# Two attention layers on one core: first-layer products alternate between query halves, first keys come from SBUF, residuals load within the block

## Chip, cores and metric

The kernel runs on one core of a Trainium2 chip. The metric is the device time of one execution in microseconds (us). Engines are named as the profile names them: PE is the tensor engine (its weight loads are shown apart, as PEld), DVE the vector engine, ACT the scalar engine, POOL GpSimd, SP the engine that issues most DMAs. SBUF and PSUM are the on-chip memories; PSUM has eight banks, and matmuls accumulate there.

## What is computed

Four images of 64 x 64 pixels and 256 channels go through two self-attention layers, each over an image's 4096 pixels ("tokens"). Cut to what matters:

```python
# layer 0
q = x @ Wq + bq;  k = x @ Wk + bk;  v = x @ Wv + bv        # 32, 32, 256 wide
x = gamma * (softmax(q @ k.T) @ v) + x
# layer 1
f = x @ Wf + bf;  g = x @ Wg + bg;  v = x @ Wh + bh        # 32, 32, 128 wide
x = x + (softmax(g @ f.T) @ v) @ Wo + bo
```

## The kernel before

**Blocks and steps.** For each image, layer 0 goes through 16 blocks of 256 queries and, within a block, through 8 steps of 512 keys. Layer 1 goes through 8 blocks of 512 queries with 16 steps of 256 keys. One object `Step` stands for one step, and a single loop (L658) goes through all of them in order.

**A step of layer 0.** `scores` (L495) makes four matmuls of 128 keys by 256 queries into the tile `st`, the only one of its kind, two PSUM banks. ACT turns it into `high` (an exponential with a slightly lowered argument, rounded to fp32r) and `p` (the plain exponential). DVE makes `low = p - high` (`cut_low`, L516) and `d` from `low` and `high` (`cut_both`, L521). These three parts of one probability are multiplied with three forms of the values, `v0h`, `v0l`, `v0d`, so that the sum has full precision from matmuls that PE takes in one go. `products_first` (L528) does this for one half `s` (128 of the 256 queries) and one part: four matmuls, one for each 128 keys (`g`), whose weights are a 128-column piece of the part and whose moving tile is `v0[..][:, g, :]`, 258 columns. A block has four accumulators of one PSUM bank each: `acc[0]` and `acc[1]` for half 0 (high and low into the first, `d` into the second), `acc[2]` and `acc[3]` for half 1. A plain step makes 24 products: high of half 0, high of half 1, low of half 0, low of half 1, then the scores of the step after next, then `d` of both halves (L714 to L724). The last step of a block has another order, so that half 0 is done early.

**The end of a block.** In layer 0, `end_first` (L563) has ACT copy `acc[0]` and `acc[2]` (L569), DVE adds `acc[1]` and `acc[3]` (L570); the next block's accumulators take these banks. In layer 1, `end_second` (L597) has ACT copy one accumulator, DVE add the other (L604), and DVE fold the running sum `p_sum` (L700) into `sums`. What follows is a list of "units": `begin` issues the loads of two residual tiles (`x_old`, from the DRAM tensor `x1_res`), `nothing` is a pause, and four `output(t)` each make two matmuls (L623, L624), a reciprocal, a DVE instruction that scales and adds the residual (L628), the store of the result, and the load of the residual tile two further on.

**Units and their pace.** Besides the outputs, units are the projections: a unit that transposes 512 tokens (in image 0 on PE, later on DVE), one for queries and keys (`qk_unit`, L408), and two to four for values (`psv`, L437). The loop spreads a block's units over its steps (L704 to L707), so a shorter list puts each unit earlier. A planner that models times orders the instructions of each engine in the end; within an engine they run in that order.

**Queries and keys.** `qk_unit` leaves `qk_parts` in SBUF (one buffer), 128 rows: high and low parts of 32 rows of q and 32 of k. SP writes it to DRAM (L428, `qk_dram`); `load_k` (L472) and `load_q` (L465) read four pieces of 32 rows back with DMAs from POOL into the tiles `k` and `q`. In image 0 the first three projections (`AHEAD`) come ahead of all steps, and the other five during the first block, three steps ahead of the step that uses them.

**Small tiles.** Residuals, outputs and other tiles of 128 x 256 share one pool `small` of four buffers.

Of the kernel before, what the change touches and what calls it, by code (L numbers as in the profile page):

```python
# [50 lines left out]
F32R = mybir.dt.float32r  # L51
# [5 lines left out]
P = 128  # L57
QB = 512
QB0 = 256
# [174 lines left out]
def fast_path(ctx: ExitStack, tc: tile.TileContext, x, w0, w1, wo, bo, gamma, out, off):  # L234
# [170 lines left out]
    def project_units(b, l, j):  # L405
        key = (b, l, j)

        def qk_unit():  # L408
            ps = side_psum(f"psqk_{b}_{l}_{j}")
            for c in range(NCC):  # L410
                for n in range(2):
                    nc.tensor.matmul(  # L412
                        ps,
                        wqk[l][:, c, :],
                        x_parts[key][c][n],
                        start=(c == n == 0),
                        stop=(c == NCC - 1 and n == 1),
                    )
            whole = data.tile([2 * D, QB], F32, tag="qk", name=f"qk_{b}_{l}_{j}")
            parts = data.tile([P, QB], F32R, tag="qk_parts", name=f"qk_parts_{b}_{l}_{j}")  # L420
            top, bottom = slice(0, 2 * D), slice(2 * D, P)
            nc.scalar.copy(whole, ps[bottom, :])  # L422
            nc.vector.scalar_tensor_tensor(whole, ps[top, :], bqk[l], whole, ALU.add, ALU.add)  # L423
            nc.scalar.copy(parts[top, :], whole)
            nc.vector.tensor_sub(parts[bottom, :], whole, parts[top, :].bitcast(F32))

            qk_dram[key] = dram.tile([2, 2, D, QB], F32, name=f"qk_dram_{b}_{l}_{j}")
            nc.sync.dma_start(qk_dram[key].rearrange("h w d n -> (h w d) n"), parts.bitcast(F32))  # L428

        per = QB // CV[l]  # L430

        def v_unit(t0):
            def issue():
                ps = side_psum(f"psv_{b}_{l}_{j}_{t0}").rearrange("p (t c) -> p t c", c=CV[l])
                for t in range(per):
                    for c in range(NCC):
                        nc.tensor.matmul(  # L437
                            ps[:, t, :],
                            xT[key][:, c, (t0 + t) * P : (t0 + t + 1) * P],
                            wv[l][:, c, :],  # L440
                            start=(c == 0),
                            stop=(c == NCC - 1),
                        )
                tiles = slice(t0, t0 + per)
                seen = [seen_v[:, l, b * NB + j, n : n + 1] for n in range(2)]
                if l == 0:
                    split_values(ps, *(v0[j][what][:, tiles, :C] for what in ("h", "l", "d")), seen[t0 // per])
                    return
                for n in range(NT // G[1]):
                    i = j * NT // G[1] + n  # L450
                    v = ps[:, n * G[1] : (n + 1) * G[1], :]
                    if split[1][i]:
                        t = data.tile([P, 3, G[1], P], F32R, tag="v1_parts", bufs=sum(split[1]), name=f"v_{b}_{i}")
                        v_t[b, i] = {what: t[:, m] for m, what in enumerate(("h", "l", "d"))}
                        split_values(v, *v_t[b, i].values(), seen[n])
                    else:
                        v_t[b, i] = data.tile([P, G[1], P], F32, tag="v1", bufs=V1, name=f"v_{b}_{i}")
                        nc.scalar.copy(v_t[b, i], v)
                        nc.scalar.activation(v, v, AF.Abs, accum_out=seen[n])

            return issue

        return [transpose_unit(b, l, j), qk_unit] + [v_unit(t0) for t0 in range(0, NT, per)]

    def load_q(b, l, j):  # L465

        q_t[b, l, j] = data.tile([P, QB], F32R, tag="q", bufs=2, name=f"q_{b}_{l}_{j}")
        for n in range(4):
            src = qk_dram[b, l, j][n // 2, 0].bitcast(F32R)
            nc.gpsimd.dma_start(q_t[b, l, j][n * D : (n + 1) * D, :], src)  # L470

    def load_k(b, l, j):  # L472

        k_t[b, l, j] = data.tile([P, QB], F32R, tag="k", bufs=NB, name=f"k_{b}_{l}_{j}")
        for n in range(4):
            src = qk_dram[b, l, j][n % 2, 1].bitcast(F32R)
            nc.gpsimd.dma_start(k_t[b, l, j][n * D : (n + 1) * D, :], src)  # L477

    def nothing():
        pass  # L480
# [5 lines left out]
    class Step:  # L486
# [38 lines left out]
                    self.d, self.low.bitcast(F32), -1.0 / EPS, self.high.bitcast(F32), ALU.mult, ALU.add  # L525
                )

        def products_first(self, acc, s, what):  # L528
            p, v, which = {
                "h": (self.high, "h", 0), "l": (self.low, "l", 0), "d": (self.d, "d", 1)  # L530
            }[what]
            for g in range(G[0]):
                nc.tensor.matmul(  # L533
                    acc[2 * s + which][:, :W],
                    p[:, g * QB0 + s * P : g * QB0 + (s + 1) * P],
                    v0[self.i][v][:, g, :],
                    start=self.first and what != "l" and g == 0,
                    stop=self.last and what != "h" and g == G[0] - 1,
                )

        def products_second(self, acc):
            v = v_t[self.b, self.i]
# [20 lines left out]
    def end_first(b, j, acc):  # L563
# [30 lines left out]

        return [residual(0), residual(1)]

    def end_second(b, j, acc, p_sum):  # L597
        key = f"{b}_{j}"
        o = []
        for h in range(QB // QB0):  # L600
            part = slice(h * QB0, (h + 1) * QB0)
            o.append(work.tile([P, W], F32, tag="o", name=f"o_{key}_{h}"))
            nc.scalar.activation(o[h][:, :QB0], acc[0][:, part], AF.Copy, scale=1.0 + EPS)
            nc.vector.tensor_add(o[h][:, :QB0], o[h][:, :QB0], acc[1][:, part])  # L604
        sums = work.tile([P, QB], F32, tag="sums", bufs=1, name=f"sums_{key}")
        nc.vector.tensor_add(sums, p_sum[:, :QB], p_sum[:, QB:])
        x_old = {}

        def load(t):
            if t < NT:  # L610
                x_old[t] = small(f"x1_old_{key}_{t}")
                nc.sync.dma_start(x_old[t], x1_res[b, j][t * P : (t + 1) * P, :])

        def begin():
            load(0)
            load(1)

        def output(t):
            def issue():
                tok = slice(t * P, (t + 1) * P)  # L620
                ps = side_psum(f"pso_{key}_{t}")
                part = o[t // NS][:, t % NS * P : (t % NS + 1) * P]
                nc.tensor.matmul(ps[:, :C], part, wo_sb, start=True, stop=True)  # L623
                nc.tensor.matmul(ps[:, C : C + 1], sums[:, tok], ones[:, :1], start=True, stop=True)  # L624
                n = (b * N + j * QB) // P + t
                nc.vector.reciprocal(inverse[:, 1, n : n + 1], ps[:, C : C + 1])
                y = small(f"y_{key}_{t}")
                nc.vector.scalar_tensor_tensor(y, ps[:, :C], inverse[:, 1, n : n + 1], x_old[t], ALU.mult, ALU.add)  # L628
                row = j * QB + t * P
                nc.sync.dma_start(out[b, row : row + P, :], y)  # L630
                load(t + 2)

            return issue

        return [begin, nothing] + [output(t) for t in range(NT)]

    def run(units):
        for u in units:
            u()


    x_res = {}
    for j in range(AHEAD):
        run(project_units(0, 0, j))
        load_k(0, 0, j)
        if j == 0:
            load_q(0, 0, 0)

    steps = [Step(b, l, j, i) for b in range(B) for l in range(2) for j in range(NQ[l]) for i in range(NI[l])]
    steps[0].scores()  # L650
# [7 lines left out]
    for n, s in enumerate(steps):  # L658
# [15 lines left out]
        if l == 0 and s.last:  # L674
            x_res[b, j] = []
            for t in range(NS):
                x_res[b, j].append(small(f"x_res_{b}_{j}_{t}"))
                row = (j * NS + t) * P
                nc.sync.dma_start(x_res[b, j][t], x[b, row : row + P, :])
                nc.gpsimd.tensor_add(x_res[b, j][t], x_res[b, j][t], bv)  # L680

        ahead = steps[n + 3] if n + 3 < len(steps) else None
        if ahead is not None and ahead.first:
# [25 lines left out]
        if l == 1:  # L709
            later.scores()  # L710
            run(todo)
            s.products_second(acc)
        else:
            for half, what in ((0, "h"), (0, "l"), (1, "h")) if s.last else ((0, "h"), (1, "h")):  # L714
                s.products_first(acc, half, what)
            for half in () if s.last else (0, 1):
                s.products_first(acc, half, "l")
            run(early[1:])
            if early:
                load_k(0, 0, s.i + AHEAD)  # L720
            later.scores()
            run(todo)
            for half, what in ((0, "d"), (1, "l"), (1, "d")) if s.last else ((0, "d"), (1, "d")):
                s.products_first(acc, half, what)  # L724

        over = (min(s.i + 2, NI[l] - 1) + 1) * G[l] // NT if j == NQ[l] - 1 else 0
        while keys and keys[0] in qk_dram and (keys[0][:2] == (b, l) or keys[0][2] < over):
# [73 lines left out]
```

## Time and profile before

| | |
|---|---|
| median of 4 runs | 3233.61 us (3231.79 to 3236.5) |
| profiled execution | 3235.59 us, of which the span of the profile is 3233.7 us |
| layer-0 block of image 1 to 3 | 27.0 to 29.2 us, by the starts of ACT's copies L569 |
| layer-1 block | 41.6 us; 37.35 us in the last image, which has no projections for a next image beside it |
| first layer-0 product of image 0; of image 1 | 33.5 us; 868.3 us |
| last layer-1 product | 3216.3 us |

A page of the profile gives, for each engine, its busy time and the number of its instructions, then the span in 40 slices with the busy share in tenths, and the clock that PE was granted. The chain that ended last names what set the end; groups of instructions are given by line, engine and tile (`acc<-v0h,high` is a matmul that reads `v0h` and has `high` as weights). In the timeline a row has its start, its length and how many instructions were merged into it; matmuls are pipelined, so the rate is read from starts, not from lengths. "Idle before" names who ended a wait.

### The profile page before, as it was taken

The numbers are of one execution on the slowest core, as the hardware profiler recorded it, in microseconds if no ns is written. First come the engines' busy times: TensorE is split into PE (matmuls) and PEld (weight loads), VectorE is DVE, ScalarE is ACT, GpSimd is POOL, SyncE is SP. The second block draws the span as 40 slices with busy tenths as digits, with TensorE's granted clock in tenths as the row PEclk, the third lists the DMA queues.
The fourth block names the chain that finished last, engine by engine and source line by source line (L and its number), as shares of the span: only waits on it lengthen the run. The fifth ranks groups of instructions, "written<-read, shape, count | busy, mean of one in ns | idle before, by whom it ended". The sixth has DMA issues, their size and how long they took to land. (4 is left out here: it accounts for less than half of the span.)

```text
span 3233.7 us, 51123 instructions
## 1 busy us (share of the span) xinstructions
PE 3172.4 (98%) x19460; PEld 2619.4 (81%) x19460; DVE 2684.5 (83%) x3181; ACT 1989.0 (62%) x2483; POOL 660.4 (20%) x784
## 2 busy tenths in 40 slices
PE   8999999999999999999999999999999999999998
PEld 7999997566699999656679999966668999995554
DVE  6788888888888888788888888878888888887776
ACT  6666666555566666565556666655555666665554
POOL 2222223000222222300022222310002222241000
PEclk9999999999999999999999999999999999999999
DMA  3112123222212112322121212222222211121111
GB/s 116 42 48 50 44 56 75 56 53 49 62 44 56 42 47 51 77 56 51 47 64 43 50 47 52 61 64 51 51 54 61 53 42 48 43 70 47 33 33 36
DMA packets 368652, 172.15 MB, mean 53 GB/s; under 512 B 257392, under 2 KB 343664, under 8 KB 368400
## 3 DMA queue, kind: packets, MB, share of 16 engines
q1 hardware_dynamic: 342528, 134.29, 16.0%
q0 software_dynamic: 24960, 34.18, 4.6%
q8 instruction: 157, 2.57, 0.3%
q14 instruction: 95, 0.78, 0.1%
q10 hardware_dynamic: 912, 0.33, 0.0%
HBM read 101.58 MB, written 67.11 MB: 52 GB/s over the span
## 5 line engine op out<-in xcount | busy, mean ns | idle before, releaser
L514 ACT ACTIVATE p<-st 128x1024 f32<-128x1024 f32 x1024 | 1044.6, 1020 | 388.3 <-PE st L502 383.3
L512 ACT ACTIVATE high<-st,down 128x1024 fp32r<-128x1024 f32 x608 | 678.7, 1116 | 691.4 <-PE st L502 573.0
L524 DVE SCALAR_TENSOR_TENSOR d<-low,high 128x1024 fp32r<-128x1024 f32 x608 | 761.2, 1252 | 209.3 <-PE acc L533 203.6
L519 DVE TENSOR_TENSOR low<-p,high 128x1024 fp32r<-128x1024 f32 x608 | 808.7, 1330 | 141.0 <-ACT p L514 141.0
L554 PE MATMUL acc<-p,v 128*128 128x512 f32 x1664 | 791.7, 598 | 0.0
L502 PE MATMUL st<-q,k 128*128 128x256 f32 (+1 forms) x3072 | 776.8, 361 | 11.4 <-ACT p L514 11.2
L700 DVE TENSOR_TENSOR p_sum<-p_sum,p 128x1024 f32<-128x1024 f32 x480 | 586.5, 1222 | 59.0 <-ACT p L514 50.7
L502 PEld LDWEIGHTS st<-q,k 128*128 128x128 f32 x3072 | 463.7, 189 | 208.6 <-ACT p L514 114.7
L533 PE MATMUL acc<-v0d,d 128*128 128x258 f32 x4096 | 592.3, 284 | 0.1
L533 PE MATMUL acc<-v0h,high 128*128 128x258 f32 x4096 | 588.5, 284 | 3.1 <-ACT high L512 3.0
L533 PE MATMUL acc<-v0l,low 128*128 128x258 f32 x4096 | 588.2, 283 | 2.3 <-DVE low L519 2.3
L533 PEld LDWEIGHTS acc<-v0h,high 128*128 128x128 f32 x4096 | 533.9, 190 | 5.3 <-ACT high L512 3.8
L533 PEld LDWEIGHTS acc<-v0d,d 128*128 128x128 f32 x4096 | 533.9, 190 | 4.8 <-DVE d L524 1.6
L533 PEld LDWEIGHTS acc<-v0l,low 128*128 128x128 f32 x4096 | 532.9, 190 | 3.9 <-DVE low L519 3.7
L554 PEld LDWEIGHTS acc<-p,v 128*128 128x128 f32 x1664 | 309.8, 190 | 226.8 <-issue 199.4
L590 POOL TENSOR_TENSOR x_res<-x,bo 128x256 f32<-128x256 f32 x128 | 215.2, 1681 | 860.4 <-DVE g L580 482.6
L470 POOL DMA_DIRECT2D q<-qk_dram x256 | 125.9, 503 | 1167.4 <-PE st L502 1145.4
L680 POOL TENSOR_TENSOR x_res<-x_res,bv 128x256 f32<-128x256 f32 x128 | 189.9, 1484 | 146.9 <-DMA x_res<-in_x 100.1
L437 PE MATMUL psv<-wv,xT 128*128 128x128 f32 (+1 forms) x1024 | 193.4, 333 | 6.7 <-DVE qk L423 6.1
L477 POOL DMA_DIRECT2D k<-qk_dram x256 | 125.2, 499 | 303.2 <-DMA qk_dram<-qk_parts 159.9
L437 PEld LDWEIGHTS psv<-wv,xT 128*128 128x128 f32 x1024 | 160.4, 193 | 30.0 <-DVE qk L423 8.7
L388 DVE TENSOR_TENSOR xl<-xT,xh 128x512 fp32r<-128x512 f32 x128 | 87.0, 682 | 4.3 <-ACT xh L387 3.9
(94 smaller groups left out, 1676.4 us busy)
## 6 DMA issues: line engine op xcount, KB each, us to landing
x_res<-in_x SPq DMA_DIRECT2D x128, 128.0 KB, 2.2
qk_dram<-qk_parts SPq DMA_DIRECT2D x64, 256.0 KB, 2.1
k<-qk_dram POOLq DMA_DIRECT2D x256, 64.0 KB, 2.1
q<-qk_dram POOLq DMA_DIRECT2D x256, 64.0 KB, 2.1
x_dram<-x SPq DMA_DIRECT2D x128, 128.0 KB, 1.7
x_res<-x_res SPq DMA_DIRECT2D x128, 128.0 KB, 1.7
squares<-x_dram SPq DMA_DIRECT2D x256, 64.0 KB, 2.3
x_old<-x_res SPq DMA_DIRECT2D x128, 128.0 KB, 2.1
```

Source lines behind the costliest of these rows:

```text
L437: nc.tensor.matmul(ps[:, t, :], xT[key][:, c, (t0 + t) * P : (t0 + t + 1) * P], wv[l][:, c, :], start=(c == 0), stop=(c == NCC - 1),)
L470: nc.gpsimd.dma_start(q_t[b, l, j][n * D : (n + 1) * D, :], src)
L502: nc.tensor.matmul(st[:, g, :], k_t[b, l, kt // NT][:, kt % NT * P : (kt % NT + 1) * P], q_t[b, l, j * n // QB][:, q0 : q0 + n], start=Tru ...
L512: nc.scalar.activation(self.high, s_flat, AF.Exp, bias=down)
L514: nc.scalar.activation(self.p, s_flat, AF.Exp)
L519: nc.vector.tensor_sub(self.low, self.p, self.high.bitcast(F32))
L524: nc.vector.scalar_tensor_tensor(self.d, self.low.bitcast(F32), -1.0 / EPS, self.high.bitcast(F32), ALU.mult, ALU.add)
L533: nc.tensor.matmul(acc[2 * s + which][:, :W], p[:, g * QB0 + s * P : g * QB0 + (s + 1) * P], v0[self.i][v][:, g, :], start=self.first and ...
L554: nc.tensor.matmul(acc[which], v[:, g, :], p[:, g * QB : (g + 1) * QB], start=first and g == 0, stop=last and g == G[1] - 1,)
L590: nc.gpsimd.tensor_add(x_old[s], x_new[s], bo_sb)
L680: nc.gpsimd.tensor_add(x_res[b, j][t], x_res[b, j][t], bv)
L700: nc.vector.tensor_add(p_sum, p_sum, s.p)
```

## The change

1. `products_first` takes a list of halves. In plain steps it is called for both halves at once, and the loop over halves is the inner one: for each 128 keys first half 0, then half 1. The last step of a block keeps its order.
2. In image 0's layer 0, `load_k`, and for the first tile `load_q`, are called within `qk_unit` and read `qk_parts` in SBUF instead of `qk_dram`. The write to DRAM stays. The calls after each projection go.
3. `load_old` loads all four residual tiles of a layer-1 block at its step 12 into four `small` tiles; the result is written in place of the residual. `begin`, `nothing` and the loads within `output` go.

```diff
@@ qk_unit
             nc.sync.dma_start(qk_dram[key].rearrange("h w d n -> (h w d) n"), parts.bitcast(F32))
+            if b == l == 0:
+                near = parts.rearrange("(h w d) n -> h w d n", h=2, w=2)
+                load_k(b, l, j, near)
+                if j == 0:
+                    load_q(b, l, j, near)
@@ loads
+    def load_rows(dst, parts, which, halves):
+        for n, h in enumerate(halves):
+            nc.gpsimd.dma_start(dst[n * D : (n + 1) * D, :], parts[h, which])
+
-    def load_k(b, l, j):
+    def load_k(b, l, j, parts=None):
         k_t[b, l, j] = data.tile([P, QB], F32R, tag="k", bufs=NB, name=f"k_{b}_{l}_{j}")
-        for n in range(4):
-            src = qk_dram[b, l, j][n % 2, 1].bitcast(F32R)
-            nc.gpsimd.dma_start(k_t[b, l, j][n * D : (n + 1) * D, :], src)
+        load_rows(k_t[b, l, j], qk_dram[b, l, j].bitcast(F32R) if parts is None else parts, 1, (0, 1, 0, 1))
@@ Step
-        def products_first(self, acc, s, what):
+        def products_first(self, acc, halves, what):
...
             for g in range(G[0]):
-                nc.tensor.matmul(
-                    acc[2 * s + which][:, :W],
-                    p[:, g * QB0 + s * P : g * QB0 + (s + 1) * P],
+                for s in halves:
+                    nc.tensor.matmul(
+                        acc[2 * s + which][:, :W],
+                        p[:, g * QB0 + s * P : g * QB0 + (s + 1) * P],
...
@@ layer 1
+    def load_old(b, j):
+
+        x_old[b, j] = []
+        for t in range(NT):
+            x_old[b, j].append(small(f"x1_old_{b}_{j}_{t}"))
+            nc.sync.dma_start(x_old[b, j][t], x1_res[b, j][t * P : (t + 1) * P, :])
+
@@ end_second
-        def begin():
-            load(0)
-            load(1)
-
...
-                nc.vector.scalar_tensor_tensor(y, ps[:, :C], inverse[:, 1, n : n + 1], x_old[t], ALU.mult, ALU.add)
+                nc.vector.scalar_tensor_tensor(y[t], ps[:, :C], inverse[:, 1, n : n + 1], y[t], ALU.mult, ALU.add)
...
-                load(t + 2)
...
-        return [begin, nothing] + [output(t) for t in range(NT)]
+        return [output(t) for t in range(NT)]
@@ the loop
+        if l == 1 and s.i == NI[1] - 4:
+            load_old(b, j)
...
-            for half, what in ((0, "h"), (0, "l"), (1, "h")) if s.last else ((0, "h"), (1, "h")):
-                s.products_first(acc, half, what)
-            for half in () if s.last else (0, 1):
-                s.products_first(acc, half, "l")
+            both = range(NS)
+            order = [((0,), "h"), ((0,), "l"), ((1,), "h")] if s.last else [(both, "h"), (both, "l")]
+            for halves, what in order:
+                s.products_first(acc, halves, what)
             run(early[1:])
-            if early:
-                load_k(0, 0, s.i + AHEAD)
             later.scores()
             run(todo)
-            for half, what in ((0, "d"), (1, "l"), (1, "d")) if s.last else ((0, "d"), (1, "d")):
-                s.products_first(acc, half, what)
+            for halves, what in [((0,), "d"), ((1,), "l"), ((1,), "d")] if s.last else [(both, "d")]:
+                s.products_first(acc, halves, what)
```

## Prediction

> **What bounds the kernel now.** I read the page first: busy shares, the clock row, the chain. Then busy time by stage, then the timeline of one layer-0 block boundary, of one layer-1 block, of the first 105 us and of the tail.
>
> ```profile
> PE 3172.4 (98%) x19460; PEld 2619.4 (81%) x19460; DVE 2684.5 (83%) x3181; ACT 1989.0 (62%) x2483; POOL 660.4 (20%) x784
> ...
> PEclk9999999999999999999999999999999999999999
> ```
>
> TensorE is busy nearly always at full clock, so an edit pays only if it shortens a matmul or fills a hole on PE. By stage (us, busy time and instructions of each engine, granted clock, DMA share, GB/s):
>
> ```profile
> 0.00:15.00 15.00, 10.25 (x28) 6.86 (x28) 5.89 (x63) 6.30 (x13) 7.85 (x18) 1.00 0.74 228
> 15.00:33.50 18.50, 15.16 (x64) 11.05 (x64) 11.75 (x18) 12.44 (x26) 8.04 (x17) 0.91 0.52 143
> ...
> 86.00:101.70 15.70, 11.18 (x69) 10.00 (x68) 8.29 (x9) 8.21 (x12) 1.94 (x4) 0.89 0.13 34
> ...
> 868.30:1320.00 451.70, 451.70 (x3732) 449.63 (x3731) 384.90 (x434) 293.33 (x357) 126.16 (x122) 1.00 0.20 50
> 525.00:868.00 343.00, 335.12 (x1111) 201.46 (x1110) 286.13 (x346) 200.60 (x258) 36.64 (x70) 0.99 0.24 58
> ```
>
> A later image's layer 0 (868 to 1320) has no hole at all: PE 451.70 of 451.70. Layer 1 (525 to 868) misses 8 us in 343. The holes lie in the first 102 us: 4.8, 3.3 and 4.5 us in the three stretches shown, the last two at a clock of about 0.9.
>
> Next, layer 0 from one block of queries to the next (start, length; PE and DVE rows):
>
> ```profile
> 1003.76 0.64 PE L502 MATMUL st<-q,k 128*128 128x256 f32 x4
> ...
> 1004.23 1.12 PE L533 MATMUL acc<-v0d,d 128*128 128x258 f32 x8
> ...
> 1005.19 0.65 PE L533 MATMUL acc<-v0h,high 128*128 128x258 f32 x4
> ...
> 1008.12 0.65 PE L533 MATMUL acc<-v0d,d 128*128 128x258 f32 x4
> 1008.30 0.42 DVE L570 TENSOR_TENSOR o<-o,acc 128x258 f32<-128x258 f32 x1
> ...
> 1008.61 1.12 PE L533 MATMUL acc<-v0h,high 128*128 128x258 f32 x8
> ...
> 1009.32 0.39 ACT L569 ACTIVATE o<-acc 128x258 f32<-128x258 f32 x1
> 1009.45 1.04 PEld L533 LDWEIGHTS acc<-v0l,low 128*128 128x128 f32 x8
> 1009.57 1.13 PE L533 MATMUL acc<-v0l,low 128*128 128x258 f32 x8
> ```
>
> Lengths overlap in the pipeline, so I read starts: eight products from 1004.23 to 1005.19 are 120 ns each; four scores from 1003.76 to 1004.23 are 118 ns each.
>
> **Alternating the halves.** The same 12,288 products, weights and bytes; only the order changes, in 7 of 8 steps (448 steps x 24 = 10,752 products). Before, four products in a row go into one accumulator and the value tile moves on each time; after, each value tile streams twice and the accumulator changes every time. Would one product get shorter? The scores bear on both points: their moving tile (q) is the same four times running, and they add to nothing (start and stop on each). They cost 118 ns for 256 columns against 120 for 258; two columns in 256 account for 0.9 ns. So neither a repeated moving tile nor the absence of accumulation buys anything visible. The last step of a block, whose order goes by half and part, gives the other bound: its 24 products take 0.98 + 0.48 + 1.46 = 2.92 us (1005.19 to 1006.65, then 1007.15 to 1008.61), a plain step's 1.95 + 0.96 = 2.91. I take 0, with 0.5 ns a product as bound each way: 10,752 x 0.5 = 5.4 us.
>
> A rule of the Trainium skill speaks against this edit. The row: the clock stays at 1.00 in all layer-0 stretches of images 1 to 3, where banks already change every four products, and falls (0.91, 0.89) only in windows where PE has holes. The rule ("TensorE: Matmul & The Clock Gate", section "A second HAM failure mode: psum-queue depth-cycling"): cycling through PSUM banks can leave small idle gaps between groups, so that the clock oscillates. The trace has no such gaps; what it would cost stands with the rivals.
>
> **The new wait.** A block's first products need accumulators that the previous block's results have left. The wait lists of both programs agree: the first product waits for ACT's copy, the first one of the second half for DVE's add L570. Before, that is the fifth product, 0.48 us in; after, the second, 0.12 us in. In the boundary above the add ends at 1008.71, 0.11 us after the first product's start at 1008.61. I followed all 60 such boundaries: in 29 (those with a projection in the block) the add ends about 0.11 us after that start, in 31 it ends 0.28 us before it. A stalled `d` product in layer 1 shows the way from a DVE end to the weight load (52 ns) and from there to the product (107 ns). So the second product starts at 0.11 + 0.05 + 0.11 = 0.27 instead of 0.12: 0.15 us, 29 times, +4.3 us. Behind it on PE stands everything else, so nothing hides it. Bounds: 0 (if only the matmul, not its weight load, waits) and 29 x 0.27 = 7.8.
>
> **Keys from SBUF.** Image 0's eight key tiles and first query tile skip the trip through DRAM: the trace has SP's write at 15.83 and POOL's key issue at 18.36, 2.5 us. An SBUF-to-SBUF transfer isn't in the trace; by the rows it lands within 1.7 to 2.9 us, and I take the 2.1 of the keys now. POOL issues the same 4 + 4 transfers at 0.5 us each. The single `qk_parts` buffer is now held until they have read it, about 4 us of a 10 us period: covered. The gain is in the order that the planner makes of it: scores of step 0 now stand before the third projection's products instead of among them, and step 6's before the last value products instead of behind. (a) Step 0's 28 x 0.12 = 3.4 us of work can fill the 3.3 us hole before 33.5, less what its two exps (2.1 us) delay the projection's ACT work: I take 2.5. (b) From 86 to 102 PE waits for `high` of step 6 (1.8 us) and its `low` (1.0); both now run beside 2.3 us of other products: 2.8. With fewer holes some of the 15.7 x 0.11 = 1.7 us lost to the clock returns: 1.2. The waits for step 7 (1.2, 0.5) stay: key tile 7 is last. Sum -6.5; bounds -9.5 (all holes of (a) and (b), all the clock) and +2 (a worse interleaving, one projection's wait of 1.5 us more).
>
> **Residuals within the block.** Four loads of 128 KB leave SP at step 12 of each layer-1 block instead of at and after its end; nothing waits behind them, since the four `small` buffers have been free since the outputs some five steps earlier. `begin` and `nothing` go from the list, so outputs come two steps earlier. In the tail one wait is tied to them:
>
> ```profile
> 3220.79 0.48 DVE L628 SCALAR_TENSOR_TENSOR y<-pso,inverse,x_old 128x256 f32<-128x256 f32 x1
> ...
> 3222.27 0.48 DVE L628 SCALAR_TENSOR_TENSOR y<-pso,inverse,x_old 128x256 f32<-128x256 f32 x1 [0.99 <-DMA x_old<-x_res]
> ```
>
> The last `y` could follow its reciprocal at 3220.71, so start at about 3220.75: -1.5 us, all of it on the path (bounds -1 and -1.6). Inside layer 1, the first output now stands behind one of the two products of step 0. After the last product of a block PE has the scores (0.47) and that product (0.86): it reaches the output at 1.3 us. The `o` add follows step 1's `p_sum` on DVE, which ends 0.7 us after that product, and needs 0.42: 1.1 us. Cover 0.2 us, so 0; the outputs' own matmuls only move. Bounds per block -0.1 and +0.1, 31 blocks: 3 us each way. What is late next there is `d` of step 12 (0.4 us a block), untouched.
>
> **Sum.** 0 + 4.3 - 6.5 - 1.5 + 0 = -3.7 us. The profiled execution took 3235.59 (span 3233.7 and 1.9 around it), so 3231.9; the median 3233.61 lies 2.0 below it, so **3229.9**.
>
> **Rivals.**
> Alternation helps after all: a product gets 1 ns or more shorter, -10.8 us a ns. For: scores of 256 columns take 118 ns and layer 1's of 512 take 233, so by that line one of 258 should take 119, and a plain step's products take 2.91/24 = 121; the accumulator or the moving tile may cost the 2. Against: in the row above, products around a change of accumulator are no shorter. At 1.5 ns: 3214. Chance 0.16.
> Slower, the early output stalls: if the `o` add ends 1.25 us or more after the block's last product, PE stands, in order, with all of layer 1 behind it. For: cover is 0.2 us, and one transpose on DVE (0.70) ahead of the add uses it up; against: DVE's order in the changed program has the add right behind `p_sum`. At 0.5 us each, 31 blocks: +15.5, 3245. Chance 0.08.
> Slower, the new order itself costs: 1 ns a product: 3241. Chance 0.06.
> The clock gate opens and shuts in layer 0: at 0.89, as at the prologue's end, 4 x 452 x (1/0.89 - 1) = +223 us, 3453. That is the clock-gate page's rule. Chance 0.02.
> It doesn't do what it says, keys arrive earlier but PE waits for ACT and DVE as before: +6.5, 3236. Chance 0.08.
> My forecast: 0.60.
>
> **From this the numbers.** 0.2% (6.5 us) is about what a measurement of this kernel can tell from no change: 3227.1 to 3240.1. My forecast's own bounds put a third of it below 3227.1. So faster 0.2 + 0.16 + a little of the prologue's upper bound: 0.39; slower the three slower rivals: 0.16; same 0.45. Range: 1.5 ns of gain at the low end, and at the high end half of the slower rivals: 3214 to 3243.
>
> **What would show it.** Starts of eight alternating products still 0.96 us apart in total. A gap of 0.15 us behind a block's first product in every other block, with L570's add as releaser. First products before 33.5 us, and the second block's before 101.7. The last `y` without a DMA wait. Layer-1 blocks still 41.6 us (37.35 in the last image). Wrong if a product's time moves by over 0.5 ns, if the output shows idle time in layer 1, or if the clock falls in layer 0.

## The result, and the profile after

The changed kernel takes 3230.42 us (median of 32 runs, 3226.21 to 3231.91), the kernel before 3233.45 (52 runs, 3230.81 to 3237.38). The ratio is 0.9989, with a 95% interval of 0.9984 to 0.9994: 1.9 to 5.2 us faster, 3.0 by the medians. The profiled execution took 3229.13 us, its span 3227.4; against the profiled execution of before that is 6.5 us less, twice the difference of the medians, and a part of this section is why.

First the page of after: the busy line and the clock row.

```profile
PE 3173.8 (98%) x19460; PEld 2618.3 (81%) x19460; DVE 2691.7 (83%) x3181; ACT 1988.9 (62%) x2483; POOL 639.6 (20%) x784
...
PEclk9999999999999999999999999999999999999999
```

The same instructions in number, PE as busy as before: nothing large has moved. So the stages, in the columns and at the times at which the prediction shows them for before (us from the start; length; busy time and instructions of PE, PEld, DVE, ACT, POOL; granted clock; DMA share; GB/s):

```profile
15.00:33.50 18.50, 16.05 (x80) 12.21 (x79) 13.50 (x19) 12.90 (x27) 8.77 (x18) 0.91 0.54 146
...
86.00:101.70 15.70, 12.66 (x97) 11.57 (x96) 11.58 (x18) 8.67 (x10) 2.36 (x3) 1.00 0.16 43
...
868.30:1320.00 451.70, 451.70 (x3700) 447.64 (x3700) 384.87 (x436) 292.53 (x357) 121.34 (x123) 1.00 0.20 50
```

Read the counts beside the busy times. From 15 to 33.5 us PE now gets 80 matmuls done instead of 64, from 86 to 101.7 us 97 instead of 69, the latter at full clock instead of 0.89. But in the same 451.7 us of a later image's first layer it gets 3700 done instead of 3732: some 32 x 0.12 = 4 us of work less (a little of it is where the fixed window falls, since the image now starts earlier, and a few records that a trace can lack). Busy is 451.70 of 451.70 in both, so the loss doesn't show as idle time. The starts tell it exactly, from the first to the last first-layer product of an image, and from the first to the last layer-1 product:

| us, from the starts in the trace | before | after | difference |
|---|---|---|---|
| first product of image 0 | 33.52 | 27.68 | -5.8 |
| last first-layer product of image 0 | 524.60 | 520.51 | -4.1 |
| first layer of image 1, 2, 3 | 452.36, 452.36, 452.34 | 454.17, 454.17, 454.16 | +1.8 each |
| layer 1 of image 0, 1, 2, 3 | 343.07, 342.53, 342.82, 303.81 | 340.78, 340.79, 342.94, 301.82 | -2.3, -1.7, +0.1, -2.0 |
| last product to the end of the span | 17.4 | 15.6 | -1.8 |

The new wait, at the block boundary where it shows (start, length, instruction; PE and DVE rows):

```profile
1002.19 0.42 DVE L574 TENSOR_TENSOR o<-o,acc 128x258 f32<-128x258 f32 x1
...
1002.51 1.27 PE L537 MATMUL acc<-v0h,high 128*128 128x258 f32 x8
...
1003.62 1.12 PE L537 MATMUL acc<-v0l,low 128*128 128x258 f32 x8
```

From 1002.51 to 1003.62 the eight high products take 1.11 us; the low ones behind them take 0.96. The add L574 ends at 1002.61. Row by row, the products of this group start at 1002.512, 1002.664 and 1002.887, then every 0.12. The next weight load behind the add is the second product's:

```profile
1002.66 0.42 PEld L537 LDWEIGHTS acc<-v0h,high 128*128 128x128 f32 x3
```

It comes 0.05 behind the add, the product at once with it, and the third product starts 0.22 later instead of 0.12.

And the tail, the `y` instruction (its tile is named `x_old` now) for the last two outputs:

```profile
3215.53 0.48 DVE L629 SCALAR_TENSOR_TENSOR x_old<-pso,inverse,x_old 128x256 f32<-128x256 f32 x1
...
3215.99 0.17 DVE L628 RECIPROCAL inverse<-pso 128x1 f32<-128x1 f32 x1
3216.19 0.48 DVE L629 SCALAR_TENSOR_TENSOR x_old<-pso,inverse,x_old 128x256 f32<-128x256 f32 x1
```

The wait of 0.99 us for a residual is gone; the last one follows its reciprocal.

**What the two profiles can't tell alone.** The difference in layer 1 changes from image to image with nothing else changed. In images 0 to 2 it sits in one stretch, early in layer 1, and there the clock differs (same columns; before, then after for images 0 and 2):

```profile
555.00:575.00 20.00, 15.00 (x43) 8.88 (x42) 14.73 (x19) 9.99 (x17) 3.92 (x8) 0.83 0.34 73
```

```profile
551.00:571.00 20.00, 14.62 (x49) 8.73 (x48) 15.87 (x22) 11.11 (x18) 3.92 (x8) 1.00 0.31 67
...
2142.00:2162.00 20.00, 15.00 (x43) 8.96 (x42) 14.76 (x19) 9.99 (x17) 2.86 (x6) 0.83 0.26 53
```

PE has three holes there (1.5, 1.8 and 1.3 to 1.7 us, for DVE's `d`, DVE's `qk` and ACT's `p`). In image 1 of before they stand in brackets, each ahead of the matmul that waited:

```profile
1353.85 0.73 PE L554 MATMUL acc<-d,v 128*128 128x512 f32 x2 [1.54 <-DVE d L524]
...
1362.47 2.00 PE L437 MATMUL psv<-wv,xT 128*128 128x256 f32 x8 [1.84 <-DVE qk L423]
...
1366.64 0.74 PE L502 MATMUL st<-q,k 128*128 128x512 f32 x2 [1.71 <-ACT p L514]
```

In the trace's clock record the clock stands at one half for 3.41 us, or twice that, within this stretch in images 0, 1 and 2 of before, and in image 2 alone of after. With it, 43 matmuls fit in 20 us, without it 49. So part of the 6.5 us between the profiles may be the luck of the clock. The experiments had to part this from the change.

### The profile page after: what moved, and what is told of

Its sections match the earlier page's. It is cut to its first block, busy times and chain, and to the rows that moved or that the text cites. A ratio compares the mean times of both kernels' runs of the same rounds, so it can differ in the third digit from the quotient of the medians.

```text
span 3227.4 us, 51144 instructions
## 1 busy us (share of the span) xinstructions
PE 3173.8 (98%) x19460; PEld 2618.3 (81%) x19460; DVE 2691.7 (83%) x3181; ACT 1988.9 (62%) x2483; POOL 639.6 (20%) x784
## 5 line engine op out<-in xcount | busy, mean ns | idle before, releaser
L527 DVE SCALAR_TENSOR_TENSOR d<-low,high 128x1024 fp32r<-128x1024 f32 x608 | 778.7, 1281 | 215.2 <-PE acc L537 208.0
L522 DVE TENSOR_TENSOR low<-p,high 128x1024 fp32r<-128x1024 f32 x608 | 791.9, 1302 | 134.0 <-ACT p L517 134.0
L594 POOL TENSOR_TENSOR x_res<-x,bo 128x256 f32<-128x256 f32 x128 | 187.9, 1468 | 917.6 <-DVE g L584 480.8
L677 POOL TENSOR_TENSOR x_res<-x_res,bv 128x256 f32<-128x256 f32 x128 | 196.8, 1538 | 112.8 <-DMA x_res<-in_x 93.1
L472 POOL DMA_DIRECT2D k<-qk_dram x224 | 109.6, 500 | 247.7 <-PE st L505 142.7
```

Of the source, the lines that this page charges most:

```text
L472: nc.gpsimd.dma_start(dst[n * D : (n + 1) * D, :], parts[h, which])
L522: nc.vector.tensor_sub(self.low, self.p, self.high.bitcast(F32))
L527: nc.vector.scalar_tensor_tensor(self.d, self.low.bitcast(F32), -1.0 / EPS, self.high.bitcast(F32), ALU.mult, ALU.add)
L594: nc.gpsimd.tensor_add(x_old[s], x_new[s], bo_sb)
```

## The experiments

All times are compared with the kernel before, run beside them on the same chip. "Image" is the length of the first layer in images 1 to 3, as in the table above; it repeats within 0.15 us from run to run, since the clock never falls there.

**Each part alone.** The first has the diff's new order of products and nothing else:

```diff
-            for half, what in ((0, "h"), (0, "l"), (1, "h")) if s.last else ((0, "h"), (1, "h")):
-                s.products_first(acc, half, what)
-            for half in () if s.last else (0, 1):
-                s.products_first(acc, half, "l")
+            order = [((0,), "h"), ((0,), "l"), ((1,), "h")] if s.last else [(both, "h"), (both, "l")]
+            for halves, what in order:
+                s.products_first(acc, halves, what)
...
```

> The kernel before with part 1 alone (halves alternate in plain steps); every other engine's order is the same as before. Theory A (read from the two profiles): each first-layer image grows by 1.8 us (452.36 to 454.17), 1.0 of it waits for the add at block boundaries, 0.8 of it 0.3 ns a product; so +7.2 us on the kernel before. Rival B (the prediction's term): only the waits, 0.14 to 0.15 us at 29 boundaries, +4.3 us. Rival C: the order shortens a product by 1 ns or more, -6 us or less.

3239.62 against 3233.26 us, ratio 1.002 (1.0011 to 1.0029): +6.4 us. Image: 454.19, 454.15, 454.13. Theory A holds; the rival of waits alone is within the interval of the time but not within that of the images. C is out. Layer 1 has its half-clock window in image 2 alone here, although nothing of layer 1 was changed. In images 0 and 1 it takes 340.82 and 340.84 us, as in the changed kernel: the 2.3 and 1.7 us that the table above has there are the clock alone.

The second loads image 0's keys and first queries from SBUF (in `qk_unit`, with the later calls taken out):

```diff
+            if b == l == 0:
+                near = parts.rearrange("(h w d) n -> h w d n", h=2, w=2)
+                load_k(b, l, j, near)
+                if j == 0:
+                    load_q(b, l, j, near)
```

> The kernel before with part 2 alone (image 0's keys and first queries from SBUF). Theory A: the first products at 27.7 us and no wait for step 6, -6 us as the prediction's term has it, seen up to the end of image 0's first layer. Rival B: a good part of the difference there was the granted clock, which stood at one half in one window of 3.4 us in the profile of before (0.89 in 86 to 101.7 us) and in none after: then -4.5 us or less. Nothing changes behind the first block in either.

3226.57 us, ratio 0.998 (0.9971 to 0.9989): -6.7 us. Its first stages, in the columns from above:

```profile
15.00:33.50 18.50, 15.46 (x84) 12.15 (x83) 13.93 (x20) 14.30 (x29) 8.49 (x18) 1.00 0.55 145
...
86.00:101.70 15.70, 12.60 (x96) 11.52 (x95) 11.57 (x17) 8.68 (x10) 2.56 (x3) 1.00 0.14 40
```

No half-clock window at all in the first 102 us, and image 0's first layer ends at 518.28. The next run is the fair comparison for that: there the keys take the old way, and no window fell either.

The third moves the residuals and drops the pauses:

```diff
+        if l == 1 and s.i == NI[1] - 4:
+            load_old(b, j)
...
-        return [begin, nothing] + [output(t) for t in range(NT)]
+        return [output(t) for t in range(NT)]
```

> The kernel before with part 3 alone (residuals loaded at step 12, outputs two units earlier). Theory A: the tail gains 1.8 us (last product to end of the span 17.4 to 15.6), layer 1's first block loses a wait of 0.8 us for ACT's p in each image, blocks of the last image 0.15 us each: -4 us in all, whatever the clock does. Rival B (the prediction's term): the tail alone, -1.5 us. Rival C: the early outputs also keep the clock up in layer 1's first block: no half-clock window there in three of three images, -8 us.

3229.29 us, ratio 0.9988 (0.9979 to 0.9997): -4.0 us, theory A's number. (Its parts as it lists them make 6.1 us; it leaves out what the later blocks of images 0 to 2 lose, 0.13 us each, see below.) Rival C is out: a half-clock window lies in layer 1's early stretch in all three of images 0 to 2 (at 555.5, 1350.8 and 2146.1 us). The last image's blocks are 37.2 instead of 37.35. Image 0's first layer ends at 522.18: 3.9 us behind the run with the keys from SBUF, both without a window. With two windows (the kernel before) it ended at 524.60. So part 2 itself is worth 3.9 us (4.7 with the version at the end of this section, whose first layer of image 0 ends at 517.51, also without a window), and each half-clock window in the first 102 us some 1.2 more. Both theories on part 2 had a piece of it.

**Parts 2 and 3 without part 1**:

```diff
-            order = [((0,), "h"), ((0,), "l"), ((1,), "h")] if s.last else [(both, "h"), (both, "l")]
+            order = [((0,), "h"), ((0,), "l"), ((1,), "h")] if s.last else [((0,), "h"), ((1,), "h"), ((0,), "l"), ((1,), "l")]
...
-            for halves, what in [((0,), "d"), ((1,), "l"), ((1,), "d")] if s.last else [(both, "d")]:
+            for halves, what in [((0,), "d"), ((1,), "l"), ((1,), "d")] if s.last else [((0,), "d"), ((1,), "d")]:
```

> The changed kernel with the old order of products (parts 2 and 3 alone). Theory A: 7 us under the changed kernel, so -10 us on the kernel before, each first-layer image of 1 to 3 back at 452.36 us. Rival B (waits alone are the price of alternation): 4.3 under the changed kernel, -7.3 on the kernel before. Rival C (the alternation helped): slower than the changed kernel, above -3 us.

3224.07 us, ratio 0.9971 (0.996 to 0.9982): -9.2 us, images back at 452.37. It beats both kernels: the alternation is a loss.

**What the alternation costs.** Of its 1.8 us an image, how much is the wait? Only a block's first high products keep the old order:

```diff
+            if s.first:
+                order[:1] = [((0,), "h"), ((1,), "h")]
```

> The changed kernel, except that the high products of a block's first step keep the old order, four of half 0 before four of half 1. Theory A (two costs): the waits at block boundaries go, 1.0 us an image, and 0.8 us an image stays as 0.3 ns a product: images 1 to 3 at 453.2 us, 4 us under the changed kernel. Rival B (waits are all): images at 452.4 us, 7 us under it. Rival C: the wait only moves to other products, no change.

3224.92 us, ratio 0.9972 (0.9962 to 0.9983). Images: 453.12, 453.11, 453.13. The same boundary as above:

```profile
1000.71 0.41 DVE L574 TENSOR_TENSOR o<-o,acc 128x258 f32<-128x258 f32 x1
...
1001.02 1.12 PE L537 MATMUL acc<-v0h,high 128*128 128x258 f32 x8
...
1001.97 0.40 PE L537 MATMUL acc<-v0l,low 128*128 128x258 f32 x2
```

Eight high products in 0.95 us (1001.02 to 1001.97) instead of 1.11. The add still ends 0.11 after the first of them, but the product that needs it is the fifth. 1.05 us an image is the wait, and 0.75 stays, as theory A said. The run beside it of the changed kernel itself took 3230.06: 5.1 us between them, 4.2 by the images.

The 0.75 us over the 2,560 products of an image that still alternate is 0.3 ns each. Two orders tell what makes it. A snake, in which the accumulator changes half as often but each value tile still streams twice:

```diff
-                for s in halves:
+                for s in halves if g % 2 == 0 else tuple(halves)[::-1]:
```

> The changed kernel, except that every second key group takes the halves in reverse (half 0, 1, 1, 0, 0, 1, 1, 0): each value tile still streams twice in a row, but the accumulator changes about half as often. If the change of accumulator is what costs 0.3 ns a product, images 1 to 3 fall by 0.4 us to 453.8; if it is the repeated moving tile or chance, they stay at 454.2. The first wait of a block stays in both. Time within 2 us of the changed kernel.

3230.13 us, ratio 0.9988 (0.9979 to 0.9997); images 454.20, 454.09, 454.13: no change, so it isn't the change of accumulator. And a crossed order, in which the accumulator changes at six of the seven passages from one product to the next in a group of eight (the expectation says seven of eight), but no value tile streams twice in a row:

```diff
-            for g in range(G[0]):
-                for s in halves:
+            pairs = [(g, s) for g in range(G[0]) for s in halves]
+            if len(halves) > 1:
+                pairs = [(g, (g + m) % 2) for m in range(2) for g in range(G[0])]
...
+                for g, s in pairs:
+                    fresh = s not in begun
+                    begun.add(s)
...
```

> The changed kernel, except that the key groups cross: groups 0 to 3 with halves 0, 1, 0, 1, then groups 0 to 3 with halves 1, 0, 1, 0. The accumulator changes on seven of eight products, but a value tile never streams twice in a row. If the repeated moving tile costs the 0.3 ns a product, images 1 to 3 fall from 454.2 to 453.4 us (the 1.05 us of boundary waits stay). If alternating the accumulators or the weights' columns costs it, they stay at 454.2.

3227.22 us, ratio 0.9979 (0.997 to 0.9988); images 453.41, 453.50, 453.45. The 0.75 us is gone and the 1.05 stays. So what cost 0.3 ns a product is the value tile that streams twice in a row: the two orders that have this cost it, and the two that don't have it don't, whether the accumulator changes at one passage in seven or at six. Why a repeat costs is not shown.

**Why layer 1 gained.** Residual loads at step 12 as in the changed kernel, but with the two pauses back:

```diff
-        return [output(t) for t in range(NT)]
+        return [nothing, nothing] + [output(t) for t in range(NT)]
```

> The changed kernel with the two pauses back at the head of layer 1's list, so that outputs come two units later as before, while the residuals still load at step 12. Theory A (the outputs' place made layer 1's gain): layer 1's first block 0.8 us longer again (waits for ACT's p back), the last image's blocks 37.35 instead of 37.2, the others 41.6 instead of 41.75: +2.3 us in all; the tail keeps its 1.8. Rival B (the loads made it): layer 1 as in the changed kernel, no change.

3232.68 us, ratio 0.9997 (0.9988 to 1.0006), 2.6 us over the changed kernel beside it. These are the waits of PE in the 56 us behind that stretch's holes in image 1 (engine, tile, line, releaser; us in total, times, longest). The kernel before has, beside 0.2 us for `d`:

```profile
PE st L502 <- ACT p L514: 0.8, 1, 0.8
```

The changed kernel has the 0.2 us alone:

```profile
PE acc L558 <- DVE d L527: 0.2, 1, 0.2
```

And this run, beside the 0.2 us:

```profile
PE st L505 <- ACT p L517: 0.8, 1, 0.8
```

The scores' wait of 0.8 us for ACT's `p` goes with the pauses and comes back with them. Theory A holds. From one block's end to the next, by ACT's copies, and where no half-clock window falls: 53.6 us for the stretch to the end of the second block instead of 52.8 (it is what the expectations call layer 1's first block, since the first outputs run in it, and it holds the early stretch above), 41.6 instead of 41.75 for the others of images 0 to 2, 37.35 instead of 37.2 in the last image. So the earlier outputs help the block that carries an image's first outputs, and the last image, and cost 0.13 us a block elsewhere; why they cost there is not shown. In images 0 to 2 the two nearly cancel. Of the 2.3 us some 2.0 are the last image's (301.8 instead of 303.8 us of layer 1).

**Is the clock luck?** Both kernels again, as they are.

> The changed kernel as it is, once more. If the half-clock windows fall by chance, by where the kernel's holes stand against a free-running period, they lie at other places than in its first profile (one at 19.6 and a double one at 2152.9 us), and stretches without one repeat within 0.1 us. If they belong to the program, they lie in the same places. The time stays at 3230, within 1.6.

3230.06 us, ratio 0.999 (0.9981 to 0.9999). Windows at 553.5 and 2942.8 us, none where the first profile had them; the stretches without one repeat within 0.1 us.

> The kernel before as it is, once more. If its first profile (five half-clock windows, one of them double) caught an unlucky phase, this one has fewer, at other places, and the profiled time lies nearer to the median 3233.5; image 0's first layer, without a window, ends near 522.2 us as in the run with part 3 alone, instead of 524.6. If the windows belong to the program, all are there again. First-layer images 452.3 us each either way.

3232.93 us, ratio 1.0002 (0.9992 to 1.0011). My expectation fell: the windows are there again, at 19.2, 90.8, 558.5, 1353.8 and 2149.1 us, and image 0's first layer ends at 524.24, not 522.2. Only the double one of the first profile is single. The half-clock windows of all profiles (ahead of the last product; a double one counts as two):

| kernel | first 102 us | images 0 to 2, early in layer 1 | image 3, same place |
|---|---|---|---|
| before, twice | 2, 2 | 4, 3 | 0, 0 |
| alternation alone | 1 | 2 | 0 |
| keys alone; residuals alone; both | 0; 0; 1 | 2; 3; 3 | 0; 0; 0 |
| changed, twice | 1, 0 | 2, 1 | 0, 1 |
| old order in the first step; snake; pauses back; crossed | 1; 0; 1; 0 | 1; 3; 3; 2 | 0; 1; 0; 1 |
| the version below | 0 | 1 | 0 |

A block with a single window lasts 1.4 to 1.7 us longer (54.4 for 52.8, 55.3 for 53.6), with a double one 2.2 (55.0, 55.8). The windows fall only in stretches where PE has holes, never in the first layer of images 1 to 3.

What decides whether a hole gets one can be read from the 13 profiles together. Within each profile all windows begin on one grid of 3.4133 us, to 0.01 us over the whole span. Where that grid stands against the kernel's first instruction differs between executions of the same program (2.49 and 0.49 us in the two profiles of the changed kernel). A grid point is a whole number of such periods away from a window's start. For the hole of 1.54 us in the early stretch, of which the profiles hold 52 (four images each), what counts is where in the grid it begins:

| hole begins, us after a grid point | holes | window |
|---|---|---|
| 0.03 to 0.39 | 5 | none |
| 0.46 to 0.64, images 0 to 2 | 5 | a double one, behind the next hole (1.84 us) |
| 0.66 to 0.76, image 3 | 3 | none (the next hole is 1.1 us) |
| 0.84 to 2.29 | 23 | a single one, from the next grid point on |
| 2.56 to 3.28 | 16 | none |

There is no exception. So it is neither pure luck nor a property of the program alone: the program sets the holes and the time from one to the next, and where the grid stands when an execution starts does the rest.

**A better version.** Parts 2 and 3 without part 1, and the pauses where they helped:

```diff
-        return [output(t) for t in range(NT)]
+        return [nothing] * (2 if j > 0 and b + 1 < B else 0) + [output(t) for t in range(NT)]
```

> Parts 2 and 3 without part 1, and the two pauses kept for blocks 1 to 7 of images 0 to 2 alone. If the places of the outputs make layer 1's differences, the first block stays at 52.8 us (or 54.4 with one half-clock window), the others of images 0 to 2 go back from 41.75 to 41.6, image 3 stays at 37.2: 2.3 us less than with parts 2 and 3 alone, -11 us on the kernel before. Rival: the difference is in the granted clock, and the time stays at -9.

3220.75 us (5 runs), ratio 0.9963 (0.9949 to 0.9977): 7.4 to 16.5 us under the kernel before, 12.2 by the medians. Blocks 41.6 and 37.2, images 452.3, early blocks 52.8 or 54.5 (with a window): as theory A had it, and the fastest kernel of this study. That it gains 3.0 on the version without the alternation instead of 2.3 is within the intervals; it also had one window in its profile where that one had four.

## Why the prediction was right, point by point

The forecast was the profiled time less 3.7 us, so a median of 3229.9; measured are 3230.42 and, again, 3230.06. The total is right, within 0.5 us. Two of its terms are too, the wait and the tail; the keys' came out at its size only with the clock's share; and the two that were put at nothing were not nothing. That these two nearly cancel (+3.0 and -2.3) is luck, and so is part of the close fit of the total.

| step | predicted | measured | by |
|---|---|---|---|
| alternation, rate of the products | 0 (up to 5.4 each way) | +3.0 | 0.75 us in each of four images, images of the fifth run against those of before |
| the new wait | +4.3 | +4.2 | 1.05 us in each of four images, changed kernel against the fifth run |
| keys from SBUF | -6.5 | -6.7 by time; -3.9 to -4.7 by the traces without half-clock windows | second run; second, and the last version, against third |
| tail | -1.5 | -1.8 | last product to the end of the span |
| outputs two steps earlier in layer 1 | 0 (up to 3 each way) | -2.3 | blocks without a window; +2.6 by time when undone |
| sum | -3.7 | -3.6 by these terms, the keys by time; -3.0 by the medians | |

**The wait** was the surest step, since it came from two rows of before (the add ends 0.11 us after the first product starts) and from who needs it. It shows at the boundaries where it was expected, 7 in each image: 28, not 29. (At the 29th, image 0's first, the add ends 0.24 us after the first product, and no product waits.) The way from the add was half right. The weight load does follow the add by 0.05 us. But its product starts with it, not 0.11 later; the loss comes on the product behind, which waits 0.22 instead of 0.12. In all 0.14 to 0.15 a boundary, as the sum had it.

**The rate** failed in the step that used the scores as witness: that a moving tile repeated four times running costs 118 ns, what its length gives, and that "neither a repeated moving tile nor the absence of accumulation buys anything visible". It buys nothing, but the witness was too coarse to see that a repeat costs: on average 0.3 ns in 120. The range around the term held it. The row to read would have been one of two equal groups of products that differ in this alone, and before had none. The rival in which the alternation shortens a product is out; the one in which it lengthens it had the right sign at a third of its size. The rival of the clock gate is out too: in seven profiles with alternating halves the clock is at full in every first layer of images 1 to 3. The rule on bank cycling in the Trainium skill ("TensorE: Matmul & The Clock Gate", section "A second HAM failure mode: psum-queue depth-cycling") doesn't apply to this stream, in which the accumulator changes at every product and PE is busy for 451.70 of 451.70 us.

**The keys** came out at the predicted size by time, but not by the predicted steps. The holes did fill: over the first 120 us PE waits 1.6 us for `high` instead of 3.0, and 0.5 for `low` instead of 2.3. These lists of waits are of before and after:

```profile
PE acc L533 <- ACT high L512: 3.0, 2, 1.8
...
PE acc L533 <- DVE low L519: 2.3, 3, 1.0
```

```profile
PE acc L537 <- DVE d L527: 1.6, 2, 1.2
PE acc L537 <- ACT high L515: 1.6, 2, 1.2
...
PE acc L537 <- DVE low L522: 0.5, 1, 0.5
```

A wait of 1.6 us for `d` has come in: the "1.2 and 0.5 for step 7" that the prediction left had company. So the two holes gave less than the 5.3 us of (a) and (b): by these rows 3.2 us less waiting and 1.6 us more, and where the remainder of part 2's gain lies is not shown. What the time has beyond it is the clock, which the prediction put at 1.2: a window costs about that, and the old way had 2, 2, 1 and 0 windows here in four profiles, the new way four in nine. How much of the 6.7 belongs to which can't be settled to better than 1 to 2 us; -3.9 to -4.7 is shown, the remainder is a count of few windows. The transfer from SBUF, for which no row of before stood, lands in 2.1 us, as taken:

```profile
k<-qk_parts POOLq DMA_DIRECT2D x32, 64.0 KB, 2.1
```

**Layer 1** was put at 0 from a cover of 0.2 us, and that cover held, if only just: 30 weight loads of outputs now wait for the `o` add (before: 2), but no matmul of an output shows idle time before it, so the rival "early output stalls" is out. What failed is that only the block's end was looked at. An image's second block had 0.8 us of waiting for ACT's `p` with nothing on PE to lie beside; with the outputs moved, that wait is gone. The prediction read no waits of that stretch, nor did it see that the last image's blocks would each get 0.15 to 0.2 us shorter and the others 0.13 longer.

**The profile against the median.** The prediction took the profiled time as base and subtracted 2.0 us for the median. That held, and the reason is in sight: the profile of before had six half-clock windows, its second profile, with five, took 3234.50 us, 1.1 less, and the first profile of the changed kernel had three.

On the clock itself, ahead of the last product the traces show lengths of 3.413 and 6.827 us only, at one half. The Trainium skill ("TensorE: Matmul & The Clock Gate", section "What's actually happening") has the same: a free-running window of 3413 ns, and nothing between half and full; the traces agree, by these lengths and by the grid above. The page's section "HAM oscillation — how this bites in real kernels" goes by idle gaps of over 3.4 us. Here the trace disagrees: no idle of PE in that stretch of layer 1 is longer than 1.85 us. Each of the 28 falls there begins at the earliest 1.1 us after the start of an idle of 1.54 us, at the latest 1.3 us after the end of one of 1.54 or 1.84 us. So part of a period is enough, if it lies at the right place in the grid; what share of it has to be idle is not settled by these runs.

Whether the alternating kernels have fewer windows (13 of 28 early layer-1 blocks, against 15 of 24 without alternation) is not shown by so few. A reason is argued: an image of the old order takes 795.3 to 795.8 us where each image has a window, and 233 periods of 3.413 are 795.3, so the next image's hole begins at nearly the same place in the grid; the 1.8 us more break that. In the run with part 3 alone it begins at 1.75, 1.75 and 1.78 us in images 0 to 2, with a window each time; in the second profile of the changed kernel at 1.35, 3.24 and 0.12, with a window in the first alone. This may be why the fifth run, 3 us longer by its images than the fourth, takes nearly the same time (their profiles have two and four windows). No run was made to test it.

## What to carry to other kernels

When the order of accumulating matmuls changes, look at who frees each accumulator: bringing the second half's first product three places forward cost 0.15 us at every boundary where its release came late, and keeping the old order in that one step gave it back. Bring matmuls into a hole rather than work on a saturated stretch; a hole on PE pays twice, once as idle time and once by the clock window that it may draw. And where profiles of one kernel differ by microseconds, count such windows first, and compare stretches without one.

## What the runs showed of the hardware that was not expected

- A 128 x 258 moving tile that streams twice in a row makes products 0.3 ns slower on average (120.4 for 120.1 ns from start to start, high and low products) than one that changes each time; changing the accumulator at six of seven passages costs nothing that the trace shows.
- A weight load that has to wait for a semaphore costs the matmul behind the next one too: starts at 0, 0.152 and 0.375 us instead of 0, 0.12 and 0.24.
- The clock falls to one half for 3.413 us, or twice that, after PE holes of only 1.5 to 1.8 us, at a cost of 1.2 to 1.7 us for a single window; whether a given hole draws it depends on where it begins in a grid of 3.413 us that runs on its own, so the same program can have it in one image and not in the next.
